# Eleven blocks searched ahead of layer 1 instead of thirteen, with three adjacency blocks summed first and loaded again

## The chip, the cores and the metric

One Trainium2 core runs the whole program in one launch. The metric is the device time of one execution in microseconds (us). The five engines are TensorE (PE; its weight loads are PEld), VectorE (DVE), ScalarE (ACT), GpSimd (POOL) and SyncE (SP); SP only issues DMAs. Each engine works through its own list of instructions in order.

## The reference

Four graph layers on N = 2708 nodes with D = 128 features, each followed by a residual and a layer norm:

```python
x = layernorm(x + (adj.T @ x) / adj.sum(axis=0)[:, None])                 # layer 0
# layer 1: messages, and an update
s = x @ msg_w[:, :D].T;  d = x @ msg_w[:, D:].T
agg = einsum('ijd,ij->id', gelu(s[:, None] + d[None] + msg_b), adj)
h = gelu(concat([x, agg]) @ upd_w.T + upd_b) + x
x = layernorm(x + layernorm(h) * ln_w + ln_b)
h = adj @ (x @ W) + b                                                      # layer 2, batch norm
x = layernorm(x + leaky(batchnorm(h), 0.2))
# layer 3: four GATv2 heads, E = leaky(x@w1 [i] + x@w2 [j])
p = exp(8 * tanh(E @ a / 8)) * adj;  out = leaky((p / p.sum(-1)) @ x @ Wlin.T)
x = layernorm(x + concat(four heads) @ w)
```

adj is 2708 x 2708 float32; its diagonal is never zero and about 0.6% of the rest is (some 16 neighbours in a row), each value between 0.05 and 1.

## The kernel before

The adjacency is handled in 22 blocks of 128 rows (21 full ones, the last, block 21, of 20 rows). A block of rows is 1354 KB. A ring of nine buffers (`RING`) holds blocks of rows.

**Head.** `take(b)` loads a block (SP's queue) and calls `count_and_sum`: PE adds the block's part of adj^T x, and of the column sums, into six PSUM banks `accs0` (27 matmuls a block: 22 column blocks, five of them split over two banks); POOL then clears the diagonal of the block in place (`affine_select`); ACT counts its nonzero entries by two passes (Sign and Relu, with accumulation). `extract(b, rows)` is the search: DVE finds the positions and values of the nonzero entries of each row, by MAX8 and FIND_INDEX8 on 16 segments, and sorts them into lists (50 DVE instructions). A buffer is free for the next load when PE, ACT and the search have read it. The loop runs over `SPLIT` = 13 blocks before layer 0, 9 blocks ahead of it in loads. `ranking` orders the searched nodes by their number of neighbours, so that a block of the sorted order has rows of like length; `lists` packs neighbours and values of a few blocks, and `place` scatters them by POOL into `lists_dram` in sorted order. `CAPS[b]` is the number of neighbours (and itself) that sorted block b provides for.

**Layer 0** (`layer0`) works in quads of four blocks: DVE normalises, PE transposes, ACT copies (`xt1`), PE multiplies by the second half of the message weights (`pm_d`), DVE adds the messages' bias (`d_sb`), and SP stores x and d to `dx_dram`.

**Layer 1** loops over the 22 sorted blocks. `own_row(b + 1)` gathers a block's own rows ahead (`x_s`); `messages(b)` gathers each neighbour's d row on POOL (`msg`, one indirect DMA a neighbour), adds s on DVE, ACT applies gelu, and DVE and PE add the weighted messages up (`own`, `parts`); `update(b)` does the rest, and POOL scatters the new rows. Nine blocks (13 to 21) are not searched in the head: they stay in the ring, and one is searched in each of the loop's first steps, two in step 0, while layer 1 runs on the first 13 sorted blocks (group 0; group 1 is the rest). Group 1's lists go out in two places, blocks 13 to 19 and then 20 and 21; `sorted_lists(1)` reads them back before group 1's first block. `transposed(e)` writes the transposed adjacency of a block to `at_dram` (PE transposes `pt_a`, ACT copies `at_sb`, SP stores in pieces of 512 bytes, seven DMAs a block); the blocks of group 0 are loaded again for it. From step 11 on, `layer2` gathers rows of `at_dram` (`at_rows`, POOL) into the same ring, and PE adds up layer 2. `load3` loads layer 3's lists on SP's queue.

**Layer 3** runs over `BLOCKS3`, 24 blocks of rows (two numbers each: chunks a row and quads), 100 quads in all, with `TOGETHER3` telling which blocks are finished together.

The order on DVE during the head and layer 0 is written out by hand (`manual_schedule`); elsewhere a scheduler orders the instructions. A queue's DMAs are issued in order, and a DMA that waits holds up those behind it. These lines of before set the order around the change:

```python
SPLIT = 13
for b in range(SPLIT):
    run(extract(b, rows_of[b]))
    if b + RING < NBLK:
        take(b + RING)
    if b == 7:
        ranking(0)
...
for _ in range(2 if b < 1 else 1):
    if left:
        e = left.pop(0)
        transposed(e, rows_of[e], True)
        run(extract(e, rows_of[e]))
```

Of the kernel before, what the change touches and what calls it, by code (L numbers as in the profile page):

```python
# [9 lines left out]
FP = mybir.dt.float32  # L10
AF = mybir.ActivationFunctionType
ALU = mybir.AluOpType
# [3 lines left out]
P = 128  # L16
N = 2708
D = 128
# [22 lines left out]
CAND = NSEG * 8  # L41
SPLIT = 13
GROUPS = [(0, SPLIT), (SPLIT, NBLK)]
CAPS = [30, 22, 20, 19, 18, 17, 16, 15, 15, 14, 13, 12, 10, 29, 20, 18, 17, 16, 14, 13, 12, 8]


BLOCKS3 = [
    *[(4, 8), (5, 6), (6, 5), (6, 5), (6, 5), (7, 4), (7, 4), (7, 4), (8, 4), (8, 4), (8, 4)],
    *[(9, 3), (9, 3), (10, 3)],
    *[(4, 3), (5, 5), (6, 4), (6, 5), (7, 3), (7, 4), (8, 4), (8, 4), (9, 3), (10, 3)],  # L50
]
# [8 lines left out]
RING = 9  # L60
LW = 2 * SLOTS + 2
BLOCKS = [(b * P, min(P, N - b * P)) for b in range(NBLK)]


ORDER = [*range(20), 21, 20]

# [8 lines left out]

TOGETHER3 = [(0, 4), (4, 8), (8, 12), (12, 16), (16, 20), (20, 23), (23, 24)]
GOT = 9
# [3 lines left out]
def gnn_resnorm_kernel(  # L81
# [31 lines left out]
    nc.gpsimd.memset(x_nat[:, :, D : D + 1], 1.0)  # L113
    nc.scalar.dma_start(
        x_nat[:, 0:NFULL, 0:D], x[0 : NFULL * P, :].rearrange("(b p) d -> p b d", p=P)
    )
    nc.scalar.dma_start(x_nat[0:NREM, NFULL, 0:D], x[NFULL * P : N, :])
# [204 lines left out]
    graph = ExitStack()  # L322
    bank = graph.enter_context(tc.tile_pool(name="bank", bufs=6, space=PSUM))
    own_ps = graph.enter_context(tc.tile_pool(name="own_ps", bufs=1, space=PSUM))
# [4 lines left out]
    with ExitStack() as layer:  # L329
# [3 lines left out]
        engine = mybir.EngineType  # L333
        hand = ExitStack()
        hand.enter_context(tc.manual_schedule(engines={engine.DVE}))

# [33 lines left out]

        ws_t = weight(msg_w[:, 0:D], "ws_t")
        wd_t = weight(msg_w[:, D : 2 * D], "wd_t")
        u1_t = weight(upd_w[:, 0:D], "u1_t")
        u2_t = weight(upd_w[:, D : 2 * D], "u2_t")
        msgb = row_on_all(work, msg_b, "msgb")
        updb = row_on_all(work, upd_b, "updb")
        lnw = row_on_all(work, ln_w, "lnw")
        lnb = row_on_all(work, ln_b, "lnb")
        w2_l2 = work.tile([P, D], FP, name="w2_l2")
        nc.scalar.dma_start(w2_l2, l2_w)  # L380

        accs0 = banks("acc0_")

        def acc_parts(jb):

            if jb >= 20:
                return [(5, (jb - 20) * (D + 1), 0, D + 1)]
            k, j = divmod(jb, 4)
            if j < 3:
                return [(k, j * (D + 1), 0, D + 1)]  # L390
            return [(k, 3 * (D + 1), 0, 125), (5, 2 * (D + 1) + 4 * k, 125, D + 1)]

        started = set()

        def load(b):
# [3 lines left out]
            return rows  # L399

        def count_and_sum(b, rows):
            r0, n = BLOCKS[b]
            for jb in [b, *(jb for jb in ORDER if jb != b)]:
                j0, m = BLOCKS[jb]
                for k, c0, f0, f1 in acc_parts(jb):
                    nc.tensor.matmul(  # L406
                        accs0[k][0:m, c0 : c0 + f1 - f0],
                        lhsT=rows[0:n, j0 : j0 + m],
                        rhs=x_nat[0:n, b, f0:f1],
                        start=k not in started,  # L410
                        stop=(b == NBLK - 1 and jb == min(4 * k + 3, 20)),
                    )
                    started.add(k)
                if jb == b:
                    nc.gpsimd.affine_select(
                        out=rows[0:n, j0 : j0 + m], in_=rows[0:n, j0 : j0 + m],
                        compare_op=ALU.not_equal, fill=0.0, base=0,
                        pattern=[[-1, m]], channel_multiplier=1,
                    )
            junk = work.tile([P, N], I8, name="junk")  # L420
            nc.scalar.activation(
                junk[0:n, :], rows[0:n, :], AF.Sign, accum_out=cnt[0:n, b : b + 1]
            )
            nc.scalar.activation(
                junk[0:n, :], rows[0:n, :], AF.Relu, scale=-1.0,
                accum_out=wrong[0:n, b, 0:1],
            )
# [246 lines left out]

        for b in range(RING):
            take(b)
            if b == 3:
                line = adj[0:1, 0:1]
                for b0, count, n in ((0, NFULL, P), (NFULL, 1, NREM)):
# [5 lines left out]
                        ),  # L685
                    )
        for b in range(SPLIT):
            run(extract(b, rows_of[b]))
            if b == SPLIT - 1:
                run(place(7, SPLIT, lists(7, SPLIT)))  # L690
            if b + RING < NBLK:
                take(b + RING)
            if b == 7:
                ranking(0)
            if b == 11:
                ranked(0)
                run(place(0, 7, lists(0, 7)))

# [3 lines left out]
        nc.vector.memset(deg, 1.0)  # L702
        deg4 = deg[:, 0:20].rearrange("p (k j) -> p k j", j=4)
        for k in range(5):
            nc.vector.tensor_copy(
                deg4[:, k, 0:3],
                accs0[k][:, 0 : 3 * (D + 1)].rearrange("p (j e) -> p j e", e=D + 1)[:, :, D],
            )
        tails = work.tile([P, 5, 4], FP, name="tails")
        nc.vector.tensor_copy(  # L710
            tails,
            accs0[5][:, 2 * (D + 1) : 2 * (D + 1) + 20].rearrange("p (k e) -> p k e", e=4),
        )
        nc.vector.tensor_copy(deg4[:, :, 3], tails[:, :, 3])
        for jb in (20, 21):
            m, at = BLOCKS[jb][1], (jb - 20) * (D + 1) + D
            nc.vector.tensor_copy(deg[0:m, jb : jb + 1], accs0[5][0:m, at : at + 1])
        nc.vector.tensor_scalar(zero, deg, 0.0, None, ALU.is_equal)
# [3 lines left out]
        nc.vector.tensor_tensor(deg, deg, zero, ALU.mult)  # L722
        part = ExitStack()
        brief = part.enter_context(tc.tile_pool(name="brief", bufs=3))

        
        def layer0(b0, count, n):
            h = brief.tile([P, 4, D], FP, name="h0")
            sums = brief.tile([P, 4], FP, name="sums0")
            var = brief.tile([P, 4], FP, name="var0")  # L730
            for j in range(count):
# [9 lines left out]
                if two:  # L741
                    nc.vector.scalar_tensor_tensor(
                        h[0:n, j, f1:D], tails[0:n, k, 0:3], deg[0:n, jb : jb + 1],
                        xs[0:n, jb, f1:D], ALU.mult, ALU.add,
                    )
                    nc.vector.tensor_reduce(sums[0:n, j : j + 1], h[0:n, j, :], AX.X, ALU.add)
# [22 lines left out]
            )  # L769
            pt = bank.tile([P, 512], FP, name="pt_x1", tag="bank")  # L770
            for j in range(count):
# [4 lines left out]
            nc.scalar.copy(xt[:, 0:w], pt[:, 0:w])  # L776
            pm = bank.tile([P, 4, D], FP, name="pm_d", tag="bank")
            for j in range(count):
# [4 lines left out]
            d_sb = brief.tile([P, 4, D], FP, name="d_sb")  # L783
            nc.vector.tensor_tensor(
                d_sb[0:n, 0:count], pm[0:n, 0:count],
                msgb[0:n].unsqueeze(1).to_broadcast((n, count, D)), ALU.add,
            )
            nc.sync.dma_start(
# [4 lines left out]
        running = []  # L793
        for quad in quads():
            running.append(layer0(*quad))
# [13 lines left out]
        msgs = layer.enter_context(tc.tile_pool(name="msgs", bufs=5))  # L809
        mine = layer.enter_context(tc.tile_pool(name="mine", bufs=2))  # L810
        tail_ps = graph.enter_context(tc.tile_pool(name="tail_ps", bufs=1, space=PSUM))
        xw = xs
# [9 lines left out]
        def messages(b, x_s, three):  # L822
# [5 lines left out]
            nc.scalar.copy(x_st[:, 0:n], po[:, 0:n])  # L828
            nc.tensor.matmul(s_ps[0:n], lhsT=x_st[:, 0:n], rhs=ws_t, start=True, stop=True)
            parts = mine.tile([P, 2, D], FP, name="parts")  # L830
# [106 lines left out]
        def layer2(b):  # L937
# [4 lines left out]
            for ib in range(NBLK) if b == 0 else ORDER:  # L942
# [7 lines left out]
                )  # L950

        again = list(range(SPLIT))
        ahead = own_row(0)
        left = list(range(SPLIT, NBLK))
        for b in range(NBLK):
# [9 lines left out]
            x_st, agg = messages(b, x_s, three)  # L965
            for _ in range(2 if b < 1 else 1):
                if left:
# [3 lines left out]
                    if e == SPLIT:  # L971
                        ranked(1)
                    if e == NBLK - 3:
                        run(place(SPLIT, NBLK - 2, lists(SPLIT, NBLK - 2)))
                    if e == NBLK - 1:
                        run(place(NBLK - 2, NBLK, lists(NBLK - 2, NBLK)))
            update(b, x_s, x_st, agg)
# [18 lines left out]
        )  # L996
        nc.vector.tensor_scalar(wrong[:, :, 4], diag, 0.0, None, ALU.is_lt)
        odd = work.tile([P, NBLK * 5], FP, name="odd")
# [1017 lines left out]
```

## Time and profile before

| what | us |
|---|---|
| median of 14 runs | 1657.52 (1650.03 to 1665.88) |
| profiled execution | 1658.08, of which the span is 1656.4 |
| first search of the head (DVE) | 19.99 |
| first h of layer 0 | 205.6 |
| first gather of layer 1 | 237.40 |
| last list of group 1 scattered | 531.07 |
| last row of layer 1 scattered | 858.60 |
| busy: PE, DVE, ACT, POOL | 1198.5, 1217.8, 700.5, 895.8 |
| mean TensorE clock granted | 0.711 of full speed |

Times in the rows from the third to the seventh are from the start of the span. In what follows, a group of instructions is given with its line, engine and operation, then the tile written and those read, the shapes, the number of instructions, the busy time and the mean, and the idle time before them with what ended it ("<-"). A line of the timeline begins with start and length. POOL's work is counted when it issues an indirect DMA, not when the data land.

### The profile page before, as it was taken

What the parts mean: (1) busy time and instruction counts of PE and PEld (TensorE: products, weight loads), DVE (VectorE), ACT (ScalarE), POOL (GpSimd) and SP (SyncE); (2) the same over time, 40 slices, a digit from 0 to 9 for tenths busy, and PEclk for the clock granted to TensorE, in tenths of its full rate; (3) what the DMA queues carried; (4) which work ended last, traced back from release to release, by engine and by line L of the source; (5) the groups of instructions that cost most, each with busy time, mean ns of one, the idle gap of its engine ahead of it and who ended that gap; (6) DMA issues with size and microseconds to landing.
All of it is one profiled execution on the core that took longest, in us unless ns stands there. A gap on an engine that the chain in (4) does not pass through costs nothing. (4 is left out here: it accounts for less than half of the span.)

```text
span 1656.4 us, 24119 instructions
## 1 busy us (share of the span) xinstructions
PE 1198.5 (72%) x5903; PEld 855.7 (52%) x5903; DVE 1217.8 (74%) x5717; ACT 700.5 (42%) x2663; POOL 895.8 (54%) x1000
## 2 busy tenths in 40 slices
PE   4996663566534565557674779898989988999994
PEld 4996652445423554546564424454545555555553
DVE  6999985777765646435534479898888988888883
ACT  2989344444323212112212534554545445555442
POOL 1000327777764777765710577765655666666530
PEclk9997655555655777767776856976776677767675
DMA  9433158888846544443411687996765765977630
GB/s 350 153 130 123 52 160 215 245 252 237 222 109 178 162 143 119 125 166 114 170 43 45 211 269 211 234 237 177 225 196 167 216 192 162 233 195 223 192 95 8
DMA packets 164355, 288.03 MB, mean 174 GB/s; under 512 B 46584, under 2 KB 118102, under 8 KB 157125
## 3 DMA queue, kind: packets, MB, share of 16 engines
q0 software_dynamic: 60496, 190.76, 41.1%
q1 hardware_dynamic: 95893, 90.69, 17.6%
q10 hardware_dynamic: 7816, 4.95, 1.1%
q8 instruction: 49, 0.80, 0.2%
q14 instruction: 101, 0.83, 0.2%
HBM read 242.28 MB, written 43.97 MB: 173 GB/s over the span
## 5 line engine op out<-in xcount | busy, mean ns | idle before, releaser
L238 POOL DMA_INDIRECT g<-t_dram,idx x400 | 402.7, 1007 | 189.7 <-issue 138.2
L238 POOL DMA_INDIRECT msg<-dx_dram,idx x368 | 348.2, 946 | 116.5 <-issue 99.1
L1308 ACT ACTIVATE sum_junk<-g 126x128 bf16<-126x128 f32 (+3 forms) x800 | 235.3, 295 | 116.8 <-DVE g L1300 63.6
L1277 PE MATMUL z<-x,copies 32*126 32x512 f32 (+3 forms) x800 | 209.3, 871 | 33.0 <-DVE g L1477 32.2
L944 PE MATMUL acc<-x_nat,at_rows 128*128 128x128 f32 (+2 forms) x968 | 156.6, 323 | 100.3 <-DMA at_rows<-at_dram,perm 99.3
L921 PE MATMUL pt_a<-ident,rows 128*128 128x128 f32 (+2 forms) x475 | 111.5, 385 | 124.8 <-ACT at_sb L926 124.2
L944 PEld LDWEIGHTS acc<-x_nat,at_rows 128*128 128x128 f32 (+2 forms) x968 | 141.9, 229 | 111.7 <-DMA at_rows<-at_dram,perm 96.8
L1477 DVE TENSOR_TENSOR g<-g,z 126x1536 f32<-126x1536 f32 (+3 forms) x100 | 174.9, 1749 | 12.1 <-PE z L1277 11.9
L406 PE MATMUL acc<-x_nat,rows 128*128 128x129 f32 (+4 forms) x1188 | 158.4, 293 | 23.0 <-DMA rows<-in_adj_dram 23.0
L406 PEld LDWEIGHTS acc<-x_nat,rows 128*128 128x128 f32 (+2 forms) x1188 | 151.7, 210 | 29.4 <-DMA rows<-in_adj_dram 24.3
L1282 PE MATMUL z<-g,ident 126*126 126x512 f32 (+3 forms) x200 | 166.1, 925 | 0.0
L921 PEld LDWEIGHTS pt_a<-ident,rows 128*128 128x128 f32 (+2 forms) x475 | 79.2, 198 | 150.4 <-ACT at_sb L926 149.4
L1308 ACT ACTIVATION_READ_ACCUMULATOR sum_junk<-g 126x1 f32 (+3 forms) x800 | 149.5, 187 | 0.0
L1354 PEld LDWEIGHTS po_s<-wm,g 126*128 126x128 f32 (+3 forms) x800 | 121.9, 237 | 41.1 <-DVE wm L1341 32.6
L1354 PE MATMUL po_s<-wm,g 126*128 126x24 f32 (+6 forms) x800 | 123.7, 309 | 24.9 <-DVE wm L1341 23.2
L1300 DVE SCALAR_TENSOR_TENSOR g<-g,a_ps 126x1024 f32<-126x1024 f32 (+3 forms) x100 | 121.2, 1212 | 0.0
L444 DVE MAX8 cv<-rows 128x8 f32<-128x170 f32 (+1 forms) x352 | 111.9, 322 | 10.0 <-DMA lnb<-in_L_gnn_ln_b_dram 10.0
L838 DVE SCALAR_TENSOR_TENSOR own<-msg,ls,own 128x128 f32<-128x128 f32 (+1 forms) x302 | 105.5, 349 | 17.4 <-ACT msg L856 15.7
L439 DVE FIND_INDEX8 ci<-cv,rows 128x8 uint32<-128x170 f32 (+1 forms) x352 | 115.8, 329 | 0.0
L926 ACT COPY at_sb<-pt_a 128x512 f32<-128x512 f32 (+3 forms) x154 | 69.6, 478 | 99.0 <-DMA at_dram<-at_sb 95.1
L1282 PEld LDWEIGHTS z<-g,ident 126*126 126x126 f32 (+3 forms) x200 | 40.9, 256 | 114.7 <-issue 89.3
L1277 PEld LDWEIGHTS z<-x,copies 32*126 32x126 f32 (+3 forms) x800 | 62.9, 240 | 71.9 <-DVE g L1477 28.2
(296 smaller groups left out, 2142.1 us busy)
## 6 DMA issues: line engine op xcount, KB each, us to landing
rows<-in_adj_dram SPq DMA_DIRECT2D x34, 1354.0 KB
at_dram<-at_sb SPq DMA_DIRECT2D x105, 256.0 KB
g<-t_dram,idx POOLq DMA_INDIRECT x400
msg<-dx_dram,idx POOLq DMA_INDIRECT x368
t_dram<-t_row SPq DMA_DIRECT2D x21, 256.0 KB
at_dram<-at_sb SPq DMA_DIRECT2D x21, 64.0 KB
dx_dram<-x_nat SPq DMA_DIRECT2D x5, 256.0 KB
dx_dram<-d_sb SPq DMA_DIRECT2D x5, 256.0 KB
```

What stands on the lines that cost most here:

```text
L238: nc.gpsimd.indirect_dma_start(out=dst, out_offset=None, in_=table[0:rows, :], in_offset=bass.IndirectOffsetOnAxis(ap=index, axis=0),)
L406: nc.tensor.matmul(accs0[k][0:m, c0 : c0 + f1 - f0], lhsT=rows[0:n, j0 : j0 + m], rhs=x_nat[0:n, b, f0:f1], start=k not in started, stop=( ...
L439: nc.vector.max_index(out=ci[0:n, at], in_max=cv[0:n, at], in_values=rows[0:n, c0 : c0 + cw])
L444: nc.vector.max(out=cv[0:n, 8 * s : 8 * s + 8], in_=rows[0:n, c0 : c0 + cw])
L921: nc.tensor.transpose(pt[0:m, j, 0:n], rows[0:n, c0 : c0 + m], ident[0:n, 0:n])
L944: nc.tensor.matmul(accs2[ib // 4][0:m, (ib % 4) * D : (ib % 4 + 1) * D], lhsT=at[0:n, i0 : i0 + m], rhs=xw[0:n, b, :], start=(b == 0 and i ...
L1277: nc.tensor.matmul(z3[0:e, r, :] if r < 3 else z1[0:e], lhsT=copies[g][rows, j, :], rhs=own[b][1][rows, :], start=True, stop=r < 3, skip_g ...
L1282: nc.tensor.matmul(z1[0:e], lhsT=ident[0:e, 0:e], rhs=g4[0:e, 3, 0:HD], start=False, stop=True, skip_group_check=True,)
L1300: nc.vector.scalar_tensor_tensor(z, z, 0.0, a_ps[0:e].unsqueeze(1).to_broadcast((e, 2, HD)), ALU.max, ALU.mult)
L1308: nc.scalar.activation(junk[0:e], g4[0:e, r, hd * D : (hd + 1) * D], AF.Identity, accum_out=sc[0:e, r, hd : hd + 1],)
L1354: nc.tensor.matmul(po[:, p0 * HEADS : (p0 + g) * HEADS], lhsT=g4s[i][0:e, r, HD : HD + D], rhs=wm[0:e, 4 * i + r, :, :], start=True, stop= ...
L1477: nc.vector.tensor_tensor(z, z, z3[0:e], ALU.add)
```

## The change

- `SPLIT` goes from 13 to 11, with new `CAPS`, `BLOCKS3` (26 blocks, 99 quads) and `TOGETHER3`.
- Blocks are taken in the order 0, 1, 2, 19, 20, 21, 3, ..., 18. Blocks 19, 20 and 21 are summed, cleared and counted, not searched, and their buffers are given to the next blocks; they are loaded and cleared again (`searched_again`) for their search in layer 1, block 19 before the loop and 20 and 21 in its step 0.
- The sums lie in seven banks, three column blocks in each, so that only the short block is split over two (23 matmuls a block). The pool of these banks is closed before layer 1, which opens its own six.
- The searches of layer 1: two in each of steps 0 and 1, then one. Group 1's lists go out in three places, blocks 11 to 15, 16 to 19, 20 and 21.
- The messages' bias is added by PE to the block's own term, as a matmul of one row, in place of DVE's add in layer 0; `d_sb` is then a copy on ACT. Layer 0 takes the short block first and its tiles `h`, `sums` and `var` have five buffers in place of three.
- x is loaded in two pieces; the loads and transposes of the weights stand behind the first takes; the diagonal is read after two takes, not four; a test of the diagonal moves from layer 2 into the head.

```diff
-SPLIT = 13
+SPLIT = 11
-CAPS = [30, 22, 20, 19, 18, 17, 16, 15, 15, 14, 13, 12, 10, 29, 20, 18, 17, 16, 14, 13, 12, 8]
+CAPS = [30, 22, 20, 18, 17, 16, 15, 14, 13, 12, 11, 30, 21, 19, 18, 17, 16, 15, 14, 13, 11, 8]
+AGAIN = 19
+TAKEN = [*range(3), *range(AGAIN, NBLK), *range(3, AGAIN)]
-TOGETHER3 = [(0, 4), (4, 8), (8, 12), (12, 16), (16, 20), (20, 23), (23, 24)]
+TOGETHER3 = [(0, 4), (4, 8), (8, 12), (12, 16), (16, 20), (20, 24), (24, 25), (25, 26)]
...
+    for b0, b1 in ((0, 3), (3, NFULL)):
+        nc.scalar.dma_start(
+            x_nat[:, b0:b1, 0:D], x[b0 * P : b1 * P, :].rearrange("(b p) d -> p b d", p=P)
+        )
...
-        accs0 = banks("acc0_")
+        accs0 = [sums_ps.tile([P, 512], FP, name=f"acc0_{i}", tag="bank") for i in range(7)]
         def acc_parts(jb):
-            if jb >= 20:
-                return [(5, (jb - 20) * (D + 1), 0, D + 1)]
-            k, j = divmod(jb, 4)
-            if j < 3:
-                return [(k, j * (D + 1), 0, D + 1)]
-            return [(k, 3 * (D + 1), 0, 125), (5, 2 * (D + 1) + 4 * k, 125, D + 1)]
+            if jb == NFULL:
+                return [(0, 3 * (D + 1), 0, 125), (1, 3 * (D + 1), 125, D + 1)]
+            return [(jb // 3, jb % 3 * (D + 1), 0, D + 1)]
...
-        for b in range(RING):
-            take(b)
-            if b == 3:
+        taken = list(TAKEN)
+        for i in range(RING):
+            take(taken.pop(0))
+            if i == 1:
...
             if b == SPLIT - 1:
-                run(place(7, SPLIT, lists(7, SPLIT)))
-            if b + RING < NBLK:
-                take(b + RING)
-            if b == 7:
+                run(place(6, SPLIT, lists(6, SPLIT)))
+            for _ in range(4 if b == 2 else 1):
+                if taken:
+                    take(taken.pop(0))
+            if b == 5:
                 ranking(0)
-            if b == 11:
+            if b == SPLIT - 2:
+                nc.vector.tensor_scalar(wrong[:, :, 4], diag, 0.0, None, ALU.is_lt)
                 ranked(0)
-                run(place(0, 7, lists(0, 7)))
+                run(place(0, 6, lists(0, 6)))
...
-            nc.vector.tensor_tensor(
-                d_sb[0:n, 0:count], pm[0:n, 0:count],
-                msgb[0:n].unsqueeze(1).to_broadcast((n, count, D)), ALU.add,
-            )
+            nc.scalar.copy(d_sb[0:n, 0:count], pm[0:n, 0:count])
...
-        for quad in quads():
+        for quad in [(NFULL, 1, NREM), *quads()[:-1]]:
...
-            nc.tensor.matmul(s_ps[0:n], lhsT=x_st[:, 0:n], rhs=ws_t, start=True, stop=True)
+            nc.tensor.matmul(s_ps[0:n], lhsT=x_st[:, 0:n], rhs=ws_t, start=True, stop=False)
+            nc.tensor.matmul(
+                s_ps[0:n], lhsT=ones[0:1, 0:n], rhs=msgb[0:1, :], start=False, stop=True
+            )
...
+        def searched_again(b):
+            rows, (r0, n) = load(b), BLOCKS[b]
+            clear_diagonal(rows[0:n, r0 : r0 + n], n)
+            return rows
+        rows_of[AGAIN] = searched_again(AGAIN)
...
-            for _ in range(2 if b < 1 else 1):
+            for _ in range(2 if b < 2 else 1):
...
-                    if e == NBLK - 3:
-                        run(place(SPLIT, NBLK - 2, lists(SPLIT, NBLK - 2)))
-                    if e == NBLK - 1:
-                        run(place(NBLK - 2, NBLK, lists(NBLK - 2, NBLK)))
+                    for e0, e1 in ((SPLIT, 16), (16, 20), (20, NBLK)):
+                        if e == e1 - 1:
+                            run(place(e0, e1, lists(e0, e1)))
+            if b == 0:
+                for e in range(AGAIN + 1, NBLK):
+                    rows_of[e] = searched_again(e)
```

## The prediction

> **What bounds the kernel now.** I read first the timeline of the page, then the table of windows by stage, then the waits of POOL and of the stretch 480 to 510, and last the timelines of DVE and POOL around the ends of stages. The page's timeline (a digit is a tenth busy in a slice of 41.4 us):
>
> ```profile
> PE   4996663566534565557674779898989988999994
> DVE  6999985777765646435534479898888988888883
> POOL 1000327777764777765710577765655666666530
> PEclk9997655555655777767776856976776677767675
> DMA  9433158888846544443411687996765765977630
> ```
>
> The head (slices 1 to 5) is DVE's. Layers 1 and 2 (slices 6 to 20) have no engine at 9: POOL's 7 is a full queue, as the window table says. Its columns are the length, then busy us (and instructions) of PE, PEld, DVE, ACT and POOL, the clock, the DMA share and GB/s.
>
> ```profile
> 83.00:124.00 41.00, 41.00 (x357) 39.36 (x356) 40.86 (x241) 34.12 (x28) 1.92 (x6) 1.00 0.35 128
> 165.00:205.00 40.00, 28.62 (x159) 27.08 (x159) 38.10 (x224) 17.00 (x14) 13.42 (x16) 0.67 0.15 52
> 237.00:300.00 63.00, 25.66 (x117) 19.01 (x114) 40.57 (x196) 28.83 (x58) 46.61 (x50) 0.56 0.85 230
> 300.00:360.00 60.00, 34.44 (x145) 26.43 (x146) 44.77 (x240) 25.92 (x61) 45.37 (x49) 0.58 0.89 246
> 480.00:530.00 50.00, 17.67 (x82) 14.77 (x82) 22.11 (x133) 11.87 (x30) 28.88 (x30) 0.57 0.50 129
> ```
>
> In the head DVE is always busy. In 237 to 360 POOL issues 99 gathers in 123 us, 1.24 us each: 0.94 of work and 0.30 of "issue", back to back. There POOL is the bound, DVE is at 0.69, and the DMA engines at 0.85 to 0.89. Starts and lengths from the timelines:
>
> ```profile
> 19.99 0.58 DVE L444 MAX8 cv<-rows 128x8 f32<-128x170 f32 x2 [9.99 <-DMA lnb<-in_L_gnn_ln_b_dram]
> ...
> 32.68 0.56 DVE L444 MAX8 cv<-rows 128x8 f32<-128x170 f32 x2
> 237.40 0.99 POOL L238 DMA_INDIRECT x_s<-dx_dram,perm  x1 [33.24 <-DVE cv L444]
> ...
> 531.07 0.90 POOL L246 DMA_INDIRECT lists_dram<-lists,rank  x1 [1.86 <-DVE wrong L631]
> 858.60 0.90 POOL L246 DMA_INDIRECT x_dram<-x_n,perm  x1 [15.17 <-DVE x_n L312]
> ```
>
> So a search is 12.7 us (19.99 to 32.68); the first gather of layer 1, which I call T0, starts at 237.4; the last list of the second group leaves at 531.1, which I call S; layer 1 ends at 858.6. S to the end is 327.5 us. The waits of 480 to 510 (us in total, times, longest):
>
> ```profile
> PE pt_a L921 <- ACT at_sb L926: 30.4, 1, 30.4
> ACT at_sb L926 <- DMA at_dram<-at_sb: 22.0, 3, 21.0
> ```
>
> SP's queue stood before its loads of layer 3's lists, which wait for a list scatter; the at_dram stores behind them stood too, so ACT had no at_sb, PE no pt_a, and DVE waited 24.4 us for PE's own. That is one price of a search late in layer 1.
>
> **The head, part by part.** The profiled execution is 1658.08 us: a span of 1656.4 and 1.7 around it, 0.56 above the median, so sums against it stand for the median too. 0.2% is 3.3 us, about what a measurement of this kernel tells from no change.
>
> - Two searches leave the head: 2 x 12.7 = -25.4 us on DVE, which has no gap there.
> - The start: x comes in two pieces and the weight loads are issued later, but PE's first instruction is still the transpose of the message weights, whose load lies behind all of x on ACT's queue; it landed at 18.7 and the first search followed at 19.99. Between 0 and -10 (the DVE setup ends at 9.99); I take -1.8, since one row load less runs beside x.
> - Sums: 23 matmuls a block, not 27, in seven banks. The blocks' first sums stand 6.22 apart at full clock; estimate 23/27 x 6.22 = 5.3. PE was full until 124 and DVE still never waited, so this is hidden, but for the tail: DVE waited 0.9 and 0.7 for the last block's sums at 202. The last block is now 18, loaded when search 9 has read its rows (140), summed before 159, ahead of search 10's end.
> - The tail from the last search to the first h took 191.5 to 205.6, 14.1 us, with six blocks' lists and 14 pairs of the next search between them; five lists, 11 pairs at 0.6 and no wait make about 9: -5. The lists taken with the ranking shrink from seven blocks to six: -2.
> - New wait: ranking now follows search 5, when blocks 0 to 10 must be counted, and blocks 19 to 21 are counted before 3. ACT takes 5.2 us a block (pair of passes); the 14th block's count is ready at about 96, where DVE wants it at 93 to 96. Before, the slack was 20. Between 0 and +8; I take +3. Behind it stand all later searches.
> - Layer 0: DVE's five d_sb adds (3.5 us busy, 3.3 waiting for pm_d) go to ACT as copies; the short block goes first. -2 to -7, -6 taken; the copies cost ACT 5 x 0.585 by the row of xt, beside DVE's work, and 3 us more if ACT is what ends.
>
> The page "ScalarE: Activation LUTs" of the Trainium skill, section "Rules for kernel authors", speaks against that: adds and simple passes belong on VectorE, and an ACTIVATE is budgeted at 0.3 us plus 0.83 ns per element, an estimate of 0.72 us for 512. This trace has 585 ns for the ACT copy and 695 for the DVE add, so the move is not dearer here; by the page it would cost ACT 0.7 us more in all and the sum would stand.
>
> T0 = 237.4 - 25.4 - 1.8 - 5 - 2 + 3 - 6 = 200.2, that is -37 us.
>
> The clock also enters: it was 1.00 while PE was full and 0.67 in 165 to 205, where the last block's sum took 12.1 us. A PE with fewer matmuls idles earlier. At 0.5, a block costs 10.6 us, less than the 12.7 of a search, so it stays hidden.
>
> **Layer 1.** What left the head comes back: eleven searches, not nine, before group 1's lists. In the changed program's order the first gather is POOL's 57th and the last list scatter its 280th: 223 x 1.25 = 279 us, and 18 of stalls as before (10.2 before an x_s, the rest at list scatters): S at 497 if POOL decides. DVE issues 1088 instructions from its first index conversion to the last list, against 894. The 894 were 205 us busy and 87 idle. Two searches add 25.4, the other 94 instructions (a further block's messages and spreads) 94 x 0.21 = 20: 250 busy. With all 87 of idle time S is 200 + 337 + 2 = 539; without the 24.4 of the SP stall 515. DVE is now later than POOL in either case. I take 520, nearer the low end, because 21.4 of the idle time was waiting for POOL's msg gathers, which a late DVE does not wait for. So of -37 at T0, -11 is left at S: the lists of group 1, which had 50 us of slack before their first use (538 to 590), become the end that POOL waits for, since x_s of block 11 stands four POOL entries behind the last scatter.
>
> From S on POOL has as many entries as before (227). Seven at_rows gathers, formerly all after S, now stand ahead of it, so PE's layer 2 sums start sooner; they were behind POOL's waits of 14.2 us before x_s. I take -5 (0 to -14). The list load must land before block 11: +3 (0 to +7). End of layer 1: 520 + 327.5 - 5 + 3 = 845.5, -13.1.
>
> Costs at nothing here: 22 bias matmuls of one row, 0.44 us each by pm_d's row, on PE that is at 0.41 to 0.57 in these windows; x_s is gathered a block ahead, which hides them, and 10 us if not. Three reloads (1354 KB land in 5.7 us alone) against one row load fewer elsewhere, cleared on POOL between gathers; the wait for 20 is asked at T0+40 and its load issued at T0+2, so 38 us cover it. If DMA is too full they hold POOL's gathers: 0 to 10. The spare buffers of sums and h take no time.
>
> **Layer 3.** 99 quads for 100, 26 blocks for 24. A line through the 23 blocks of before gives 5.84 us a quad and 3.0 a block: -5.8 + 6.0, so 0; -7 to +8.
>
> Sum: 1658.1 - 13.1 = 1645.
>
> **The rivals.**
> - A: POOL stays the bound, DVE catches up. S = 497, end 822, -36: 1622. For it: DVE at 0.69 had room. Against: its idle time is chains through PE and ACT, not spare time. 0.20.
> - B: the head gives less. Key wait 8, no earlier start, tail and lists -4, layer 0 -2: T0 = 214, 14 later: 1659, no change. For it: the slack of ACT's counts. 0.10.
> - C, slower: SP's queue stalls once more. The lists now leave in three places, not two, and SP's loads of layer 3's lists stand ahead of the at_dram stores at each. A second stall like 480 to 505 adds 24 us to DVE's path: S = 520 + 25 = 545, end 545 + 325.5 = 870.5, +12: 1670, and 1675 with the upper list load. It decides as soon as S is later than 533. The at_rows gathers ahead of the last scatter make it dearer: the first waits for all at_dram stores, and the lists queue behind it on POOL. 0.25.
>
> The page "TensorE: Matmul & The Clock Gate", section "What's actually happening", says that an idle window of about 3.4 us puts the array back to half clock; the windows above fit that, 1.00 when full and 0.56 when 0.41 busy. By it PE's share of every chain in layer 1 would stay as it was, and the sum with it; a PE kept fuller by extra transposes would gain clock.
>
> **How the numbers follow.** My forecast, S between 508 and 530, has 0.45 and runs from 1633 to 1655. With A and C the range is 1617 to 1675. Faster: A's 0.20 and 0.38 of the forecast; same: 0.07 of it and 0.03 of B; slower: C's 0.25 and 0.07 of B.
>
> **What would show it.** Right: T0 near 200; no wait of over 8 us of DVE before 100; S near 520 with POOL waiting 15 to 30 us for DVE just before it; the end of layer 1 near 846; layer 3 as long as before. A shows S below 505 and no such wait. C shows PE's pt_a waiting 20 us or more for at_sb in two places. I am wrong in kind if T0 is later than 220, if the head's searches have gaps, or if POOL stalls at a reload.

## The result and the profile after

The changed kernel takes 1678.59 us (median of 10 runs, 1675.4 to 1689.03), against 1659.19 for the kernel before in the same comparison: a ratio of 1.0128, interval 1.0106 to 1.0149. It is about 20 us slower (19.4 between the medians, 21 by the ratio), where 1645 was predicted. Its profiled execution is 1680.1 us with a span of 1678.3.

The same landmarks as in the table of before, in us from the start of the span:

| landmark | before | predicted | after |
|---|---|---|---|
| first search | 19.99 | 18.2 | 16.79 |
| first h of layer 0 | 205.6 | 174.4 | 188.9 |
| T0, first gather of layer 1 | 237.4 | 200.2 | 223.6 |
| S, last list of group 1 | 531.1 | 520 | 546.8 |
| last row of layer 1 | 858.6 | 845.5 | 879.3 |
| from there to the end of the span | 797.8 | 797.8 | 799.0 |

The gain at the head is 13.8, not 37, and between T0 and S it turns into a loss. The page's timeline after:

```profile
PE   6696435564575813464786749998889989989985
DVE  7959966776878551545553557887879887888985
POOL 1000257767653577777600577665657657675641
PEclk9898565655556956777776857676787786776775
DMA  8623258986867433434411577775767658776650
```

In the head DVE's third digit has fallen from 9 to 5 (84 to 126 us), and in slices 11 to 14 POOL's 7 6 4 7 has become 6 5 3 5. Three windows of after, with the columns named in the prediction, answer to those of before:

```profile
83.00:124.00 41.00, 39.17 (x325) 38.08 (x326) 20.69 (x122) 37.95 (x34) 2.05 (x7) 0.92 0.22 74
300.00:360.00 60.00, 32.75 (x151) 24.73 (x152) 47.25 (x255) 25.82 (x62) 44.93 (x48) 0.64 0.92 259
480.00:530.00 50.00, 25.91 (x116) 19.25 (x114) 38.23 (x216) 19.81 (x49) 23.77 (x25) 0.60 0.59 148
```

In the first, DVE is busy for 20.69 of 41 us, where it was for 40.86. The second is as before. In the third DVE has 38.23 where it had 22.11: it is now the fullest engine ahead of S, and POOL has 25 instructions in place of 30. The timeline of DVE in the head, the rows after a wait of more than 2 us from 10 to 130:

```profile
16.79 0.58 DVE L439 MAX8 cv<-rows 128x8 f32<-128x170 f32 x2 [6.80 <-DMA lnw<-in_L_gnn_ln_w_dram]
113.28 0.17 DVE L491 SCALAR_TENSOR_TENSOR key<-cnt,nkey 128x11 f32<-128x11 f32 x1 [20.28 <-ACT junk L416]
```

The second row is the new wait of the ranking: 20.28 us for ACT's counts, where the prediction had 3 with bounds of 0 and 8. The timeline of ACT, first of before and then of after, shows where the counts were held:

```profile
31.59 0.39 ACTq L680 DMA_DIRECT2D diag<-in_adj_dram  x1
...
34.21 7.44 ACTq L680 DMA_DIRECT2D diag<-in_adj_dram  x1
...
41.77 2.46 ACT L421 ACTIVATE junk<-rows 128x2708 int8<-128x2708 f32 x1 [5.02 <-issue]
```

```profile
15.90 0.39 ACTq L676 DMA_DIRECT2D diag<-in_adj_dram  x1
...
16.80 25.80 ACTq L676 DMA_DIRECT2D diag<-in_adj_dram  x1
...
42.65 2.46 ACT L419 ACTIVATE junk<-rows 128x2708 int8<-128x2708 f32 x1 [22.48 <-issue]
```

The diagonal is read on ACT's queue in two DMAs, 2708 pieces of four bytes in all: first the 2688 of the 21 full blocks (10.5 KB), then the 20 of the last block (0.1 KB). The issue of the large one takes 0.39 us in both kernels. The row that is held is that of the small one right behind it: 25.8 us instead of 7.4. ACT does nothing behind it: after its first counting pass it stands 22.5 us. In both kernels this issue ends at about 42 (34.21 + 7.44 and 16.80 + 25.80). The windows of after say what ends there:

```profile
30.00:42.00 12.00, 12.00 (x108) 11.69 (x107) 12.00 (x73) 0.00 (x0) 0.58 (x2) 1.00 0.99 348
42.00:50.00 8.00, 8.00 (x66) 7.83 (x66) 8.00 (x46) 7.32 (x6) 0.19 (x1) 0.90 0.52 165
```

The DMA share falls from 0.99 to 0.52 at 42: the burst of x and the first nine row loads is over. The pieces of the diagonal went out mostly at its end: of all DMA packets under 512 bytes, 777 fall in the 23.5 us from 16.5 to 40 and 2051 in the 3 us from 40 to 43. ACT's column is 0.00 in the first row.

ACT reaches the read at 15.9 instead of 31.6, ahead of the first counting pass. Two lines of the change can have brought it forward: the diagonal is read after two takes, not four, and the weights' transposes and copies, which stood ahead of it on ACT in before (the copies at 19.19 to 31.45), now stand behind the takes. No run separates the two.

The timeline of POOL at T0, S and the end of layer 1:

```profile
223.61 0.99 POOL L244 DMA_INDIRECT x_s<-dx_dram,perm  x1 [31.35 <-DMA at_dram<-at_sb]
...
541.88 0.99 POOL L252 DMA_INDIRECT lists_dram<-lists,rank  x1 [7.93 <-DVE rs_t L272]
...
546.84 0.90 POOL L252 DMA_INDIRECT lists_dram<-lists,rank  x1 [2.71 <-DMA lists_dram<-lists,rank]
...
562.72 0.95 POOL L244 DMA_INDIRECT x_s<-dx_dram,perm  x1 [10.88 <-issue]
...
879.31 0.89 POOL L252 DMA_INDIRECT x_dram<-x_n,perm  x1 [10.28 <-DVE x_n L318]
```

POOL waits for DVE and for the lists just before S, and 10.9 more before the next own rows, where before it went on.

### The profile page after: what moved, and what is told of

It is laid out like the page before. It is cut to its first block, busy times and chain, and to the rows that moved or that the text cites. A ratio compares the mean times of both kernels' runs of the same rounds, so it can differ in the third digit from the quotient of the medians.

```text
span 1678.3 us, 24090 instructions
## 1 busy us (share of the span) xinstructions
PE 1187.7 (71%) x5821; PEld 840.5 (50%) x5821; DVE 1213.5 (72%) x5746; ACT 704.5 (42%) x2679; POOL 902.2 (54%) x1003
## 5 line engine op out<-in xcount | busy, mean ns | idle before, releaser
L945 PE MATMUL acc<-x_nat,at_rows 128*128 128x128 f32 (+2 forms) x968 | 155.8, 320 | 93.4 <-DMA at_rows<-at_dram,perm 92.4
L1485 DVE TENSOR_TENSOR g<-g,z 126x1536 f32<-126x1536 f32 (+3 forms) x99 | 173.1, 1749 | 14.2 <-PE z L1285 13.8
L405 PE MATMUL acc<-x_nat,rows 128*128 128x129 f32 (+3 forms) x1012 | 131.1, 292 | 13.4 <-DMA rows<-in_adj_dram 13.4
L1362 PEld LDWEIGHTS po_s<-wm,g 126*128 126x128 f32 (+3 forms) x792 | 117.4, 231 | 39.4 <-DVE wm L1349 30.1
L1362 PE MATMUL po_s<-wm,g 126*128 126x24 f32 (+6 forms) x792 | 119.1, 304 | 23.4 <-DVE wm L1349 23.3
L405 PEld LDWEIGHTS acc<-x_nat,rows 128*128 128x128 f32 (+2 forms) x1012 | 126.0, 202 | 18.4 <-DMA rows<-in_adj_dram 14.0
```

The costliest lines, as they stand in the source:

```text
L405: nc.tensor.matmul(accs0[k][0:m, c0 : c0 + f1 - f0], lhsT=rows[0:n, j0 : j0 + m], rhs=x_nat[0:n, b, f0:f1], start=k not in started, stop=( ...
L945: nc.tensor.matmul(accs2[ib // 4][0:m, (ib % 4) * D : (ib % 4 + 1) * D], lhsT=at[0:n, i0 : i0 + m], rhs=xw[0:n, b, :], start=(b == 0 and i ...
L1362: nc.tensor.matmul(po[:, p0 * HEADS : (p0 + g) * HEADS], lhsT=g4s[i][0:e, r, HD : HD + D], rhs=wm[0:e, 4 * i + r, :, :], start=True, stop= ...
L1485: nc.vector.tensor_tensor(z, z, z3[0:e], ALU.add)
```

## The experiments

The theory: the head is late because the diagonal's read holds ACT, and what the head gains or loses goes to the end of layer 1 in full. The rivals: layer 1 ends when POOL and the lists are done whatever the head does, so that an earlier T0 buys nothing; the loss is the two searches moved into layer 1, as work of DVE; the third place of the lists, or the copies on ACT in layer 0, cost it.

Some runs fell on chips where the kernel before takes 1995 to 2020 us, not 1655 to 1659: from about 220 us on their profiles show waits named "remote", of ACT and DVE above all, that the others lack, so of those runs only the head, and differences between kernels that ran side by side, are read. One line of the waits of e1 from 230 to 600 (total, times, longest):

```profile
ACT agg_t L875 <- remote: 75.1, 6, 26.6
```

**The diagonal's read on SP's queue**, behind the nine loads (e1, repeated as e5 and e10):

```diff
-            if i == 1:
+            if i == RING - 1:
...
-                    nc.scalar.dma_start(
+                    nc.sync.dma_start(
```

> The changed kernel, with the diagonal read on SP's queue behind the first nine loads instead of on ACT's queue beside the first counts. Theory 1 (ACT is held for 22.5 us because its queue cannot take the 2709 four-byte pieces while the row loads fill the DMA engines): ACT counts without a gap from about 18, DVE's wait for the key falls from 20.3 us to 0 to 4, the first gather of layer 1 comes at 203 to 208 (223.6 in the changed kernel), and since DVE's chain from there to the last list is unchanged at 323, the whole 16 to 20 us reach the end: 1659 to 1664. Rival 1 (ACT's lag comes from the rows, or from the weights' transposes): the key wait stays over 10 us and the time over 1672. Rival 2 (POOL or the DMA engines set the last list of group 1): first gather near 205, but the last list still at 540 to 547, time over 1672.

> The kernel of e1 once more, on another chip if there is one: on the chip of e1 to e4 the kernel before took 2020 us, with waits from 210 us on that the profiles of before and changed kernel do not have, so only its head could be read. Theory 1: key wait under 6 us, first gather at 206 to 212, last list 320 to 326 us later, time 0.4 to 1.0% below the changed kernel, so a ratio to before of 1.002 to 1.009. Rival 2 (the gain of the head is lost before the last list): last list still at 540 to 547, ratio 1.011 or more.

> The kernel of e1 and e5, beside the changed kernel on one chip. Theory 1: first gather 14 us earlier than in e9, the last list earlier by as much, time 10 to 16 us below e9. Rival 2 (the gain of the head is lost before the last list): last list within 4 us of e9's, time within 4 us of it.

The head did what the theory says in all three: the key wait was 4.81, 4.63 and 0.65 us, T0 209.6, 209.6 and 206.7. The times of e1 and e5 are 2006.8 (ratio 0.9932, 0.990 to 0.9964) and 1984.8 (0.9954, 0.9925 to 0.9982) on the other chips. e10, beside e9, gives the comparison that counts: 1664.9, ratio 1.0033 (1.0011 to 1.0056). Timelines of DVE, SP and POOL in e10:

```profile
96.75 0.17 DVE L491 SCALAR_TENSOR_TENSOR key<-cnt,nkey 128x11 f32<-128x11 f32 x1 [0.65 <-ACT junk L416]
```

```profile
30.78 11.29 SPq L676 DMA_DIRECT2D diag<-in_adj_dram  x2
```

```profile
206.72 0.99 POOL L244 DMA_INDIRECT x_s<-dx_dram,perm  x1 [30.95 <-DMA at_dram<-at_sb]
...
532.68 0.90 POOL L252 DMA_INDIRECT lists_dram<-lists,rank  x1 [2.51 <-DMA lists_dram<-lists,rank]
```

The two issues on SP also end at 42 (30.78 + 11.29), but behind them stands only the next row load, which goes out at 42.30 (45.27 in after). The edit changes two things, the queue and the place in the order; which of them is needed was not tried. It also has a price at the start: the third row load goes out at 10.45 instead of 15.39, the message weights land later, and the first search begins at 19.89, 3.1 later than in after.

**The changed kernel once more** (e9), as the base of e10 to e12 on their chip.

> The changed kernel itself, beside e10 to e12. On the chips of e1 to e8 the kernel before took 1995 to 2020 us and every experiment stood below it, so it is open whether the changed kernel is slower than before there at all. On a chip like that of the first measurement: ratio 1.010 to 1.015, first gather at 223.6, last list at 547. On a chip like those of e1 to e8: first gather at 223 to 224 all the same (the head agrees between the chips), last list 415 to 427 us after it, ratio 0.998 to 1.010.

1680.0, ratio 1.0119 (1.0084 to 1.0154); T0 223.9, S 548.7, end of layer 1 882.4. Against it, e10 is 17.2 earlier at T0, 16.1 at S, 17.4 at the end of layer 1 and 15.1 in the time. Moving the read gives back 15 of the 22 us that the changed kernel loses beside e10, and the rival by which an earlier T0 buys nothing falls: what the head gains without moving work arrives.

**The message bias back on DVE** (e2, repeated as e15 and e17): the add in layer 0 as before, and no bias matmul.

```diff
-            nc.scalar.copy(d_sb[0:n, 0:count], pm[0:n, 0:count])
+            nc.vector.tensor_tensor(
+                d_sb[0:n, 0:count], pm[0:n, 0:count],
+                msgb[0:n].unsqueeze(1).to_broadcast((n, count, D)), ALU.add,
+            )
```

> The changed kernel, with the messages' bias added again by DVE in layer 0 (d_sb on DVE, no bias matmul in layer 1). Theory 1 (the move of d_sb to ACT brought nothing, because layer 0 is a chain through DVE, ACT and PE): layer 0 from first h to first gather stays within 2 us of the changed kernel's 33, time 1675 to 1681. Rival (ACT's copies made layer 0 longer): first gather 3 to 6 us earlier, time 1672 to 1675. Rival (the prediction's own step: the copies saved 6 us): first gather 5 us later or more, time 1683 or more.

> The kernel of e2 (the changed kernel with the messages' bias added by DVE in layer 0). Theory 1: the last stores of layer 0 land sooner because group 1's key is broadcast behind them; first gather at 219.5 to 221.5, 3 us ahead of the changed kernel, the last list and the time lower by 2 to 5 us: 1675 to 1678. Rival (layer 1 gains from the bias on PE what layer 0 loses): time 1679 to 1683.

> The kernel of e2 and e15 (bias on DVE in layer 0). On a chip where the kernel before takes 1657: theory 1, first gather at 219.5 to 221.5, time 1675 to 1678; rival (layer 1 gains from the bias on PE what layer 0 loses), 1679 to 1683. On a chip where it takes 1995 or more: first gather at 220 and nothing new.

T0 was 220.2, 220.2 and 216.1, that is 1.7 to 5.9 earlier than in the kernels with the copies that ran beside them and have the rest of the head alike (221.9 to 223.1), and 3.4 to 7.5 earlier than in after. In e17 layer 1 ends at 869.5, 9.8 before that of after, and its profiled execution is 1667.2; but its ratio, 1.0116 (1.0070 to 1.0161, 1674.2 us), does not stand apart from 1.0128. On the other chips the ratios are 0.9906 (0.9873 to 0.9939) and 0.9874 (0.9839 to 0.991), the best of those that ran beside them. So the copies on ACT bring nothing and probably cost some us.

**Thirteen searches with all else of the change** (e3): SPLIT, CAPS, BLOCKS3, TOGETHER3, the order of blocks and the places of lists as in before, and the diagonal on SP.

```diff
-SPLIT = 11
+SPLIT = 13
...
-TAKEN = [*range(3), *range(AGAIN, NBLK), *range(3, AGAIN)]
+TAKEN = [*range(NBLK)]
...
-            for _ in range(2 if b < 2 else 1):
+            for _ in range(2 if b < 1 else 1):
```

> The kernel of e1 (diagonal on SP) with 13 blocks searched in the head again, blocks taken in their order, nothing loaded again, and the capacities, layer 3 blocks and list groups of the kernel before; the seven banks, the split load of x, the bias on PE and the order of layer 0 stay. Theory 1 (what left the head comes back in layer 1 at full price): first gather at 226 to 234, last list 290 to 300 us after it, time 1645 to 1653, below e1 by 8 us or more. Rival (the other parts of the change make layer 1 longer, not the two searches): first gather the same, but last list 315 us or more after it, time over 1668.

T0 236.0 against 209.6 of e1 beside it, 26.4 later for two searches; but T0 to S took 382.9 against 426.5, and the times were equal: 2007.5 (0.9927, 0.9888 to 0.9966) and 2006.8. What the head gains by two searches less, layer 1 gives back.

**Message weights loaded ahead of x** (e6 with 13 searched, e7 with 11, both with the diagonal on SP):

```diff
+    first_w = [const.tile([P, P], FP, name=f"first_w{i}") for i in range(2)]
+    for i, t in enumerate(first_w):
+        nc.scalar.dma_start(t, msg_w[:, i * D : (i + 1) * D])
```

> The kernel of e3 (13 blocks in the head, diagonal on SP, the other parts of the change kept) with the two message weights loaded ahead of x on ACT's queue. Theory 1: the first search comes at 9 to 12 us instead of 16.8 to 20, the head shifts by 7 to 9, first gather at 226 to 230, last list 290 to 300 us after it, ratio to before 0.988 to 0.996: faster than both kernels. Rival (rows and x land no earlier, or the later loads set the pace): first search before 12, but first gather at 233 or later, ratio 0.998 or more.

> The kernel of e5 with the two message weights loaded ahead of x. Theory 1: first search at 9 to 12, but the key again waits for ACT's counts, which then lag by as much as DVE starts earlier (7 to 9 us more of key wait, some 12 in all); first gather at 203 to 209, last list 320 to 326 later, ratio 1.000 to 1.007. The difference to e6 is the price of two searches in layer 1: 10 us or more, e6 faster. Rival (layer 1 takes no longer for two more searches when it begins earlier): e7 level with e6 or faster.

The first search began at 12.6 and 12.7 instead of 19.9 and 20.1, T0 at 228.2 and 200.2: 7.8 and 9.4 earlier. The times are 1977.0 and 1980.3, ratio 0.9918 both: e6 was expected 10 us or more ahead of e7, and the two are level.

**Two searches left out of layer 1** (e4, repeated as e8, e13 and e16): blocks 12 and 14 get the positions found for block 11.

```diff
+                    if e in (12, 14):
+                        for found in (k1, k2):
+                            nc.vector.tensor_copy(found[:, e, :], found[:, SPLIT, :])
...
+                    else:
+                        run(extract(e, rows_of[e]))
```

> The changed kernel, with the searches of blocks 12 and 14 left out of layer 1 (their entries are copied from block 11's, so the lists are not the right ones; their lengths are counted as before). Theory 1 (DVE's chain sets the last list): the last list comes 20 to 27 us earlier than 546.8, POOL's wait before it shrinks, time 1652 to 1660. Rival (POOL or the transposed stores set it): the last list at 538 or later, time 1670 or more.

> The kernel of e4 once more (the changed kernel with the searches of blocks 12 and 14 left out of layer 1, their entries copied from block 11's). Theory 1 (DVE's chain sets the last list): last list 20 to 27 us ahead of 546.8, ratio to before 0.996 to 1.003. Rival (POOL's queue or the transposed stores set it): last list at 538 or later, ratio 1.009 or more.

> The kernel of e4 and e8 (the changed kernel with the searches of blocks 12 and 14 left out of layer 1, their entries copied from block 11's). Theory 1 (DVE's chain sets the last list, and the two searches are its longer part): from first gather to last list 296 to 303 us, 21 to 28 less than 324, time 20 to 27 below the changed kernel: 1653 to 1660. Rival (POOL's queue or the transposed stores set it): 315 or more, time 1670 or more.

> The kernel of e4, e8 and e13 (two searches left out of layer 1). On a chip where the kernel before takes 1657: theory 1 (DVE's chain), from first gather to last list 296 to 303 us, time 1653 to 1660; rival (POOL's queue or the transposed stores), 315 or more, time 1670 or more. On a chip where it takes 1995 or more: 394 to 399 as in e4 and e8, and nothing new.

If the searches' work on DVE were the loss, this should have given back most of the 20 us, and the runs do not agree. On the other chips the times are 2009.7, 1986.2 and 1981.9 (ratios 0.9956, 0.9954 and 0.9947, intervals within 0.992 to 0.9985). T0 to S takes 392 to 399 there, 409 to 427 in the other kernels with 11 searched, and e13 is 17 us below e14 beside it, which has all the searches. e16 is the one run on a chip like the first: 1681.1 (four executions), ratio 1.0158 (1.0109 to 1.0207), no gain at all. There T0 to S fell from 323.2 to 313.4, and S to the end of layer 1 grew from 332.5 to 343.1. The timelines of DVE and POOL in e16:

```profile
338.03 0.15 DVE L305 TENSOR_SCALAR ln_var<-ln_var 128x1 f32<-128x1 f32 x1 [24.04 <-ACT ln_junk L300]
```

```profile
528.41 0.97 POOL L244 DMA_INDIRECT at_rows<-at_dram,perm  x1 [13.05 <-DMA at_dram<-at_sb]
...
535.33 0.91 POOL L252 DMA_INDIRECT lists_dram<-lists,rank  x1 [3.35 <-DMA lists_dram<-lists,rank]
...
550.43 0.95 POOL L244 DMA_INDIRECT x_s<-dx_dram,perm  x1 [10.33 <-DVE rs_y L284]
```

DVE lost 24.04 us at one place, behind a stop of SP's queue (25.5 us for a list, in after 18.1): in after that stop cost DVE 8.8. It begins to pack the last list at 522.57, 12.7 us sooner behind T0 than in after (536.93). Then POOL stands 13.05 us before the first at_rows gather, which needs every store of the transposed adjacency, and the last list stands behind that gather, so that 9.9 of the 12.7 are left. On this kind of chip DVE's work alone does not explain the loss: most of what the searches freed went into a longer wait for lists and stores. This rests on one profile.

**Group 1's lists in two places, not three** (e14):

```diff
-                    for e0, e1 in ((SPLIT, 16), (16, 20), (20, NBLK)):
+                    for e0, e1 in ((SPLIT, 20), (20, NBLK)):
```

> The changed kernel with group 1's lists sent out in two places (11 to 19, then 20 and 21) instead of three. Theory 1 (the places matter little beside DVE's chain): from first gather to last list 318 to 330, time within 6 us of 1680. Rival (the third place, with its stop of SP's queue, is what makes layer 1 longer): 305 to 315, time 1665 to 1672.

1999.0, ratio 1.0017 (1.0001 to 1.0034), beside 0.9947 and 0.9874 of the two other kernels that ran with it; T0 to S 419.8, inside the 409 to 427 of the other kernels with all 22 searches and 11 of them in the head on these chips. So there the third place is not what makes the stretch long; on a chip of the first kind this was not run.

**All repairs together**, diagonal on SP, weights first and bias on DVE, with 13 searched (e11) and with 11 (e12).

> The kernel of e6 (13 blocks in the head, diagonal on SP, message weights ahead of x) with the messages' bias added by DVE in layer 0 as in the kernel before. Theory 1: the last stores of layer 0 land 3 us after the last addition, not 5 to 6, since group 1's key is then broadcast later; first gather at 224 to 226, ratio to before 0.985 to 0.994. Rival: the add puts DVE on the path, first gather at 228 or later, ratio as e6's 0.992 or above.

> The kernel of e7 (11 blocks in the head, diagonal on SP, message weights ahead of x) with the bias on DVE in layer 0. Theory 1: first gather at 196 to 199, some 27 us ahead of e11's, and all of it given back by the last list, which comes level with e11's or later; ratio to before 0.992 to 1.002. Rival (the prediction's picture: layer 1 gives back two thirds): time 5 to 10 us below e11.

Both are half a per cent faster than the kernel before, and faster than the change: 1649.8, ratio 0.9949 (0.9925 to 0.9973), and 1651.4, ratio 0.9953 (0.9928 to 0.9978). e12 has its T0 at 199.8, as was predicted for the change (but with its first search at 12.9, not 18.2), 21.7 before e11's 221.6, and no more than 3.4 us of key wait. Yet the times are level: T0 to S is 323.6 against 294.9. (The profiled execution of e12, 1657.7, is the slowest of its twelve; that of e11 is 1646.6.)

## Why the prediction was wrong, point by point

The 35 us between 1645 and 1680.1 are, by landmarks, 23.4 at T0, 3.4 from T0 to S, 7.0 from S to the end of layer 1 and 1.2 behind it (33.8 + 1.2 = 35.0).

- **New wait: the step that failed.** The term "+3, between 0 and +8" was 20.28, 17.3 too small. It was worked out from ACT's pace (5.2 us a block) and its order of before. The prediction has no term for the diagonal's read; the profile of before had the warning, 7.44 us of issue with 5.02 idle behind it, and the change moved that instruction 17 us earlier, deeper into the burst. e10, which moves only this read, has a wait of 0.65 and gives 15 us back. By the prediction's own signs this is an error in kind: T0 is later than 220, and DVE waits over 8 us before its ranking. The page "DMA: Bandwidth & Descriptors" of the Trainium skill, section "Issuing engines are not separate DMA queues", says that issuing from several engines saves only the time on the sequencer, usually small beside the DMA itself. The first half fits: the read ended no earlier on SP. The second does not hold here: the second issue of the read was held for 25.8 us, nearly until the pieces had gone, and on ACT it was on the path.
- **Start.** -1.8 was predicted, -3.2 came. Right in kind: PE's first transpose waits for the weights, and with them ahead of x the search starts at 12.6 to 12.9 (e6, e7, e12). The gain hangs on the row loads, as was argued: where the third goes out at 10.45 to 10.73 (e1, e5, e10), the start is 19.9 to 20.1 as in before, and at 15.39 (after) it is 16.8.
- **Sums, tail and lists.** A block's sums stand 5.24 apart (POOL clears blocks at 24.01, 29.25 and 34.49), 5.3 was the estimate. First h: 174.4 predicted, 17.3 of wait and -1.4 of start added make 190.3; 188.9 came. These terms, taken together, were right to 1.4 us.
- **Layer 0: the second failed step.** -6 was predicted; from first h to T0 it took 34.7 instead of 31.8, so +2.9. The last `d_sb` copy at 217.27 is only 28.4 behind the first h (29.1 in before), and the first gather comes 6.3 after it, where before needed 2.6 (234.77 to 237.40). In between, the key row of group 1 (704 KB) goes out, which before issued after T0 (240.96), and a row load (220.71; 239.61 in before):

```profile
217.27 0.27 ACT L784 COPY d_sb<-pm_d 128x128 f32<-128x128 f32 x1 [0.58 <-PE pm_d L779]
217.33 0.33 ACTq L501 DMA_DIRECT2D key_row<-key_dram  x1
```

  The same holds in all 19 profiles. In the 13 with the copies the key row goes out within 0.1 us of the start of the last copy, and T0 is 5.2 to 8.9 behind that copy; from first h to T0 they take 32.6 to 35.0. In the six with DVE's add (before, e2, e11, e12, e15, e17) the key row goes out after T0, T0 is 2.6 to 3.0 behind the last add, and the stretch is 26.8 to 31.8. So the copies made this stretch longer, not shorter as the term has it. That it is the key row which delays the last stores of d is argued from its place; no run moves it alone. (The 0.72 us that the prediction takes from the page on ScalarE is stated there for an ACTIVATE with its bias as a pointer; these copies took 0.58.)
- **T0 to S.** 319.8 was predicted, 323.2 came: the size was right. DVE was 240.9 us busy (205.8 before; 250 predicted) and 82.3 idle (87.9 before). The prediction had 539 for the case that all idle time stays, and left it for 520 on the ground that 21.4 of it was waiting for POOL; that ground fell, since nearly all the idle time stayed, and the size fits only because DVE had 9 us less to do than estimated and its worst stall shrank. The length does not depend on T0: 323 to 326 in four kernels with 11 searched (after, e9, e10, e12 between T0 = 199.8 and 223.9, and 322.6 in e17), 294 to 295 in two with 13 (before, e11). So the two searches moved, with the reloads and the sizes that go with them, cost 28.7 (e11 to e12) to 29.5 us there, and what they gain at T0 is 21.7 (e11 to e12), on the other chips 26.4 (e3 to e1) and 28.0 (e6 to e7).
- **What bounds that stretch** is less simple than "DVE". In e16 DVE was 220.0 busy, 20.9 less, and only 9.9 came through; the rest became idle time (93.4), and the one stop behind SP's queue grew by more than that, from 8.8 to 24.04. Rival C named both parts, the stop of SP's queue and the at_rows gathers ahead of the last scatter. In after, the stall that C priced came once and early: SP waited 18.1 us for a list, and PE for at_sb just behind it, but DVE lost only 8.8 there, where the stall of before cost it 24.4:

```profile
394.52 1.11 PE L922 MATMUL pt_a<-ident,rows 128*128 128x128 f32 x4 [18.56 <-ACT at_sb L927]
...
396.63 0.35 DVE L839 SCALAR_TENSOR_TENSOR own<-msg,ls,own 128x128 f32<-128x128 f32 x1 [8.80 <-ACT msg L857]
```

  No second one came, and e14 speaks against the third place of the lists. C was right on the sign; that its S of 545 was only 2 us off was luck, since it stood on a T0 of 200 and on a second stall.
- **S to the end.** 325.5 was predicted, 332.5 came. The two waits, 14.2 us together, for layer 2's sums before x_s are down to 2.01 and 3.00, as was argued for the -5; but POOL waits 10.88 before x_s at 562.72, and 37.4 in all for new rows before their scatters (26.2 in before). The row names no releaser for the 10.88; the list load was expected to cost 3 there, and e16's row names DVE instead. Which of the two it is stays open, and so does why e16's remainder is 10.6 longer (its copied lists are not excluded as a cause).
- **Layer 3.** 0 was predicted, +1.2 came.
- **Rivals.** A (POOL stays the bound) is refuted by S. B had the right place, a smaller head gain through the key wait, but stopped at 8 us.

## What to carry to other kernels

When an edit moves work away from in front of a DMA, ask where that DMA's issue now falls: a read of thousands of small pieces, issued while the DMA engines were full, held the next issue on its queue, and with it the engine, until the burst was over, so it belongs on a queue with nobody behind it. Work moved from a stage that is bound by one engine into a stage that seems to have idle time is worth only what that stage's chains let through: here (e11 to e12) two searches less ahead of layer 1 brought its first gather 21.7 us forward and made the next stretch 28.7 longer. Test the split by itself: with the same repairs on both sides it brought nothing.

## What the hardware showed that was not expected

The issue of a read of 2688 four-byte pieces took 0.39 us, and the issue of 20 pieces right behind it on the same queue 25.8, 7.4 and, on SP, 7.0 us (35.06 to 42.07 in e10), by when it began; it ended at about 42 each time, when the row loads' burst did. With the weights ahead of x the burst ends later, and so does the issue (43.24 in e12). x's loads show the same: the issue of x's last 20 rows, right behind the large load, took 9.06 us in after. Chips differ: the kernel before takes 1655 to 1659 us on some and 1995 to 2020 on others, whose profiles show waits named "remote" from about 220 us on, while T0 of one and the same head agrees within 2.0 us (the changed one), 2.9 (diagonal on SP) and 4.1 (bias on DVE). On those chips the experiments that ran on both kinds had ratios of 0.987 to 0.996 where they had 1.003 to 1.016 on the first kind; the changed kernel itself was not run there.
